# A tuned perceiver layer: who asks for the experts' weights, how many pairs are held at a time, and where the gathered results go

## The chip, the cores and the metric

The kernel runs on one core of a Trainium2 chip. The metric is the device time of one execution in microseconds (us), the median over several runs. Engines are TensorE (PE; PEld is its weight load), VectorE (DVE), ScalarE (ACT), GpSimd (POOL) and SyncE (SP). All numbers are float32.

## The reference, cut to what matters

One layer has three parts, each added to the 256 x 512 latents `x`: attention of the latents over themselves and 4096 context rows, a state-space mixer, and a mixture of experts. The change lies in the last part:

```
x      = layernorm(latents)                        # 256 tokens, 512 wide
scores = sigmoid(x @ gate_w)                       # 32 experts
w, i   = top_k(scores, 6);  w = w / sum(w)
routed = sum over the 6 experts e of a token: w_e * ((silu(x @ wg[e]) * (x @ wu[e])) @ wd[e])
shared = (silu(x @ sg) * (x @ su)) @ sd
out    = latents + routed + shared
```

An expert has 512 x 192 weights for `wg`, as many for `wu`, and 192 x 512 for `wd`.

## The kernel before, in words

The kernel is written in a tile framework: the programmer allots tiles from pools and writes the instructions; the framework sets each engine's order and all semaphores. `tc.issue_after(i)` puts an engine's instructions behind `i` on the same engine. Each engine runs its own list in order.

**Attention and mixer** take the first 785 us or so. Their tile `xn` (2 x 512 values per partition) holds normalised rows, in between the target of ACT's sums of squares (line 282) and the zeros that are written to DRAM; `xT` (4 x 256) is its transpose, in between room for sums.

**Routing** (from about 785 us). `route`, `ranks` and `counts` give each token's six experts. `places` orders the 24 experts behind the first eight by how many tokens they have and draws them into 24 slots; the slot's expert number comes out of a matmul into `ps_place`, is copied to `expert` (line 1272) and turned by `place_rows` into row numbers `place` for gathers. `result_rows` finds where a token's results will stand (`row_y`), and `list_later` which tokens belong to a block (`listed`).

**Units.** The 32 experts are worked off as 16 pairs, here called units 0 to 15 (`NP`). Units 0 to 3 are the eight fixed experts; 4 to 15 are drawn at run time. A unit's weights are two tiles of 1024 KB, one for each expert (gate, up and the first 128 rows of down; `WEX` = 2048 values per partition), and one of 256 KB with the remaining down rows of both. `NHELD` = 6 places in SBUF hold the weights of six units; the places are buffers of finished work, collected by `hold`. `load_pair(n)` puts unit n's weights into place n mod 6. For the fixed experts SyncE copies them (`load_weights`, line 1406); for the drawn ones GpSimd issues three indirect gathers through `place` (`rows_at`, line 1394).

**The loop** (lines 1765 to 1803) does in round n: `gate_up(n)` (L237 for units 0 to 4, whose two experts have separate blocks of 128 token rows; L1629 for units 5 to 15, whose two experts share one block), `fetch` of token rows (`xg_sb`, gathers on GpSimd from DRAM `xd`), `turn(n + 1)` (TensorE transposes L1601, DVE copy `xgT` L1603), `down(n - 1)` (L1700, L1703, or L1651, L1652), `load_pair(n - 1 + NHELD)`, and `turn_hidden(n)`. Units 4 and 5 are loaded before the loop.

**Results.** Up to unit 10 a block's result `y_sb` is stored to DRAM `ye` by ACT's queue (L1708, L1660). The last five units (from `LAST` = 11) stay on chip: `spread` adds them into `total` by a matmul (L1670). The stored ones are gathered back per token, six gathers `yk` for each of two token tiles (L1557), and added to `x_sb` with their weight on DVE (L1565, `add_behind`). The first tile's six use the pool `yp` of six buffers; the second tile's use four of the same and two of `xg`'s. At the end `finish` adds `total` (L1811) and SyncE stores the output (L1814). If an expert has more tokens than its block has room (`crowded`), another, slower arm runs; the profiled execution did not take it.

Of the kernel before, what the change touches and what calls it, by code (L numbers as in the profile page):

```python
# [23 lines left out]
KD = DM // P  # L24
# [42 lines left out]
NSLOT = NE - FIXED  # L67
# [17 lines left out]
def perceiver_layer(ctx: ExitStack, tc: tile.TileContext, a: dict, out: bass.AP):  # L85
    nc = tc.nc
# [35 lines left out]
    ident = const.tile([P, P], FP, name="ident")  # L122
# [27 lines left out]
    def layer(ctx, bounded):  # L150
# [6 lines left out]
        keep = ctx.enter_context(tc.tile_pool(name="keep", bufs=1))  # L157


        xn = keep.tile([P, NT, DM], FP, name="xn")  # L160
        xT = keep.tile([P, KD, L], FP, name="xT")
        oacc = keep.tile([P, NT, NKV, REP * P], FP, name="oacc")
        lacc = keep.tile([P, NT, NKV, REP * P], FP, name="lacc")

# [3 lines left out]
        row = keep.tile([P, NT, TOPK], U32, name="row")  # L168
        row_y = keep.tile([P, NT, TOPK], U32, name="row_y")
        place = keep.tile([P, NPL], U32, name="place")  # L170
        listed = keep.tile([P, NB], U32, name="listed")
        token = keep.tile([P, NT], FP, name="token")
        crowded = keep.tile([1, 1], I32, name="crowded")
# [1075 lines left out]

        def places(pc):  # L1250

            pos, key, keys, at, value, drawn = (
                m[n] for n in ("pos", "key", "keys", "at", "value", "dst"))
# [12 lines left out]
            ps = bank("ps_place")  # L1266
            TE.matmul(ps[:, 0:n], number, slot[:, 0:n], start=True, stop=True)
            V.tensor_tensor(drawn[:, :, 0:n + 1], m["table"], two(slot, n + 1), ALU.mult)
            V.tensor_reduce(value, drawn[:, :, 0:n + 1], AX.X, ALU.add)
            V.tensor_tensor(drawn, two(ident[:, 0:NE], NE), value.unsqueeze(2).to_broadcast([P, 2, NE]), ALU.mult)  # L1270
            TE.matmul(ps[:, NE:3 * NE], ones, drawn.rearrange("p a b -> p (a b)"), start=True, stop=True)
            V.tensor_copy(expert, ps[:, 0:n])
            place_rows()
            V.tensor_copy(m["base"], ps[:, NE:3 * NE].rearrange("p (a b) -> p a b", b=NE))
# [117 lines left out]
        def rows_at(out, src, c, by=place):  # L1392

            return G.indirect_dma_start(out=out, out_offset=None, in_=src,  # L1394
                                        in_offset=bass.IndirectOffsetOnAxis(ap=by[:, c:c + 1], axis=0)).ins
# [6 lines left out]
        def load_weights(to, n, fixed, behind=None):  # L1402

            if fixed:
                for i in range(2):
                    wait_for(nc.sync.dma_start(to[i], a["experts"][2 * n + i]), behind)
                nc.sync.dma_start(to[2], a["down_rest"][2 * n:2 * n + 2].rearrange("e p n -> (e p) n"))
            else:
                s = 2 * n - FIXED
                for i in range(2):  # L1410
                    rows_at(to[i], a["experts"].rearrange("e p n -> (e p) n"), s + i)
                return rows_at(to[2], a["down_rest"].rearrange("e p n -> (e p) n"), NE - FIXED + s // 2)

        def load_pair(n, behind=None):
            if n < NP:
                k = n % NHELD
                weights[n] = (held[2 * k], held[2 * k + 1], rests[k])
                return load_weights(weights[n], n, 2 * n < FIXED, behind)

# [129 lines left out]

        def gather(src, rows, t, rings):

            got = []
            for k, (pool, tag) in enumerate(rings):
                yk = pool.tile([P, DM], FP, tag=tag, name="yk")
                G.indirect_dma_start(out=yk, out_offset=None, in_=src,  # L1557
                                     in_offset=bass.IndirectOffsetOnAxis(ap=rows[:, t, k:k + 1], axis=0))
# [150 lines left out]

        with ExitStack() as rctx:  # L1710
            main = Rounds(rctx, weights)
            yp = rctx.enter_context(tc.tile_pool(name="yp", bufs=6))
            idx, rowf, sc, rank, mask, iota = (m[n] for n in ("idx", "rowf", "gate", "rank", "mask", "iota"))
            spread, = carve(m["kv", 0], (TAIL // 2, L))

# [31 lines left out]

            for n in range(2):
                begun = main.fetch(n)
            for n in range(FIXED // 2, NHELD):  # L1750
                with tc.issue_after(begun):
                    begun = load_pair(n)
            copied = main.turn(0)
            with tc.issue_after(copied):
                rows_in_blocks(at)
            fetched = {0, 1}
            got, r_x, r_k = [], [(main.e4, "xg")], [(yp, "yk")]

            def add_behind(n, k0, k1):

# [4 lines left out]
            for n in range(NP):  # L1765
                gate_up(n)
                if n == 0:
                    list_later(main.ps_x.tile([P, KD * P], FP, tag="x", name="ps_list"))

                for f in range(n + 2, NP):  # L1770
                    if f not in fetched and sum(main.blocks(b) for b in range(n + 1, f + 1)) <= 4:
                        with tc.issue_after(begun):
                            begun = main.fetch(f)
                        fetched.add(f)

                if n + 1 < NP:
                    main.turn(n + 1)
                if 0 < n <= LAST:
                    down(n - 1)
                elif n > LAST:  # L1780
                    main.down_here(n - 1)
                if n == LAST:
                    got.append(gather(ye, row_y, 0, r_k * TOPK))
                elif n == LAST + 1:
                    total = [main.ps_ye.tile([P, DM], FP, tag="ye", name="total") for _ in range(NT)]
                    got.append(gather(ye, row_y, 1, r_k * 4 + r_x * 2))
                if n > LAST + 1:
                    spread_last(n - 2)
                if n >= NP - 3:
                    add_behind(n, *{NP - 3: (0, TOPK), NP - 2: (TOPK, 2 * TOPK - 2), NP - 1: (2 * TOPK - 2, 2 * TOPK)}[n])  # L1790
                if n > 0:
                    load_pair(n - 1 + NHELD)
                if n == 0:
                    with tc.issue_after(begun):
                        for z in main.zeroed:
                            G.memset(z, 0.0)
                    with tc.issue_after(main.done[n]):
                        room()
                if n == 2:
                    with tc.issue_after(main.done[n - 1]):  # L1800
# [19 lines left out]
            with arms.Else():  # L1820
# [2 lines left out]
                dst, row2f, row2 = m["dst"], m["m8"][:, :, 0:TOPK], row_y  # L1823
                xg_rows = dram_disjoint_views(xg, NT * TOPK)
                for t in range(NT):
                    V.tensor_scalar(dst[:, t], iota[:, 0:NE], float(L), None, ALU.mult)
                    V.tensor_tensor(dst[:, t], dst[:, t], rank[:, t], ALU.add)
                    V.tensor_tensor(own[:, 0:TOPK], m["hot"][:, t], dst[:, t].unsqueeze(1).to_broadcast([P, TOPK, NE]), ALU.mult)
                    V.tensor_reduce(row2f[:, t, :], own[:, 0:TOPK], AX.X, ALU.add)
                    V.tensor_copy(row[:, t, :], row2f[:, t, :])  # L1830
                    for k in range(TOPK):
                        G.indirect_dma_start(
                            out=xg_rows[t * TOPK + k], in_=xn[:, t, :], in_offset=None,
                            out_offset=bass.IndirectOffsetOnAxis(ap=row[:, t, k:k + 1], axis=0))
# [15 lines left out]
                V.tensor_scalar(row2f, row2f, float(NE * L), None, ALU.min)  # L1850
                V.tensor_copy(row2, row2f)
                for t in range(NT):
                    add(gather(ye2, row2, t, [(main.e4, "xg")] * TOPK), t)
                    store(t)

    flag = nc.values_load(small_scores, min_val=0, max_val=1)
# [54 lines left out]
```

## Time and profile before

| what | us |
|---|---|
| median of 3 runs | 940.52 (939.85 to 940.58) |
| the profiled execution | 946.23 |
| its span, first to last instruction | 944.3 |
| TensorE busy | 924.2 |
| first L237 of unit 0 | starts at 810.04 |
| first L1629 (unit 5) | starts at 860.66 |
| last `total` matmul ends | 937.90 |

The span is 1.9 us shorter than the profiled execution's own time. A profile line such as `L1629 PE MATMUL ps_egu<-w_in,xgT` reads: line of the kernel, engine, operation, tile written, tiles read. In a timeline the brackets behind an instruction tell how long its engine was idle before it and what released it. In the chain of waits each piece has its start, its length and what ran.

### The profile page before, as it was taken

The numbers are of one execution on the slowest core, as the hardware profiler recorded it, in microseconds if no ns is written. First come the engines' busy times: TensorE is split into PE (matmuls) and PEld (weight loads), VectorE is DVE, ScalarE is ACT, GpSimd is POOL, SyncE is SP. The second block draws the span as 40 slices with busy tenths as digits, with TensorE's granted clock in tenths as the row PEclk, the third lists the DMA queues.
The fourth block names the chain that finished last, engine by engine and source line by source line (L and its number), as shares of the span: only waits on it lengthen the run. The fifth ranks groups of instructions, "written<-read, shape, count | busy, mean of one in ns | idle before, by whom it ended". The sixth has DMA issues, their size and how long they took to land.

```text
span 944.3 us, 10567 instructions
## 1 busy us (share of the span) xinstructions
PE 924.2 (98%) x3266; PEld 504.9 (53%) x3266; DVE 577.4 (61%) x1199; ACT 370.0 (39%) x853; POOL 427.8 (45%) x498
## 2 busy tenths in 40 slices
PE   7999999999999999999999999999999999999996
PEld 3444555555555555555555555554465775654332
DVE  4866766566666665756666656658588685661224
ACT  4556444344344343443444434434154442022121
POOL 3769846345544644724725544220013251545542
PEclk9999999999999999999999999999999999999999
DMA  9651053053024114204305203090025481779983
GB/s 331 203 112 58 1 179 89 1 154 92 1 66 146 33 31 159 57 3 154 90 0 157 68 1 89 14 298 1 0 101 197 145 309 68 288 287 348 421 330 101
DMA packets 129716, 122.33 MB, mean 130 GB/s; under 512 B 79889, under 2 KB 99122, under 8 KB 124402
## 3 DMA queue, kind: packets, MB, share of 16 engines
q1 hardware_dynamic: 118960, 77.43, 27.2%
q0 software_dynamic: 7504, 39.59, 11.3%
q10 hardware_dynamic: 3186, 4.54, 1.3%
q8 instruction: 28, 0.46, 0.2%
q14 instruction: 38, 0.31, 0.1%
HBM read 89.54 MB, written 32.00 MB: 129 GB/s over the span
## 4 chain that ended last, share of the span: by engine, by line
PE 96%; DVE 2%; DMA 0%; issue 0%; ACT 0%; POOL 0%; SPq 0%; ACTq 0%
PE oT L774 24%; PE scT L748 24%; PE ps_kv L522 16%; PE ps_self L237 4%; PE ps_egu L1629 3%; PE ps_o L969 3%; PE ps_egu L237 3%; PE ps_first L399 3%; PE ps_xbc L237 2%; PE ps_out L1163 1%; PE ps_z L237 1%; PE xgTp L1601 1%; PE ps_ye L1651 1%; PE ps_ye L1652 1%; PE total L1670 1%; PE ps_ye L1700 1%
## 5 line engine op out<-in xcount | busy, mean ns | idle before, releaser
L765 DVE TENSOR_TENSOR lacc<-lacc,prT 128x512 f32<-128x512 f32 x256 | 199.8, 781 | 198.0 <-ACT prT L754 196.6
L754 ACT ACTIVATE prT<-scT,bq,rk 128x512 f32<-128x512 f32 x256 | 198.4, 775 | 280.9 <-PE scT L748 268.8
L748 PE MATMUL scT<-qT,kT 128*128 128x512 f32 x536 | 273.5, 592 | 0.0
L774 PE MATMUL oT<-prT,v 128*128 128x512 f32 x528 | 269.4, 592 | 0.0
L774 PEld LDWEIGHTS oT<-prT,v 128*128 128x128 f32 x528 | 100.2, 190 | 125.3 <-issue 118.6
L748 PEld LDWEIGHTS scT<-qT,kT 128*128 128x128 f32 x536 | 101.3, 190 | 41.4 <-issue 30.8
L522 PE MATMUL ps_kv<-fast,ctx 128*128 128x256 f32 x350 | 99.5, 379 | 0.0
L522 PEld LDWEIGHTS ps_kv<-fast,ctx 128*128 128x128 f32 x350 | 66.5, 190 | 47.9 <-issue 39.9
L471 POOL TENSOR_TENSOR ctx<-ctx 128x128 f32<-128x128 f32 x21 | 10.4, 495 | 98.7 <-PE ps_kv L522 98.7
L211 POOL TENSOR_TENSOR rk<-pv,mhalf 128x4 f32<-128x4 f32 x32 | 38.7, 1219 | 27.3 <-DVE pv L210 27.1
L522 PE MATMUL ps_kv<-wkv,ctx 128*128 128x256 f32 x168 | 48.8, 379 | 0.0
L282 ACT ACTIVATE xn<-kraw 128x128 f32<-128x128 f32 x112 | 33.5, 301 | 38.5 <-POOL kraw L497 21.5
L507 POOL TENSOR_TENSOR v<-fast,v 128x768 f32<-128x768 f32 x21 | 40.8, 1958 | 16.5 <-DVE fast L551 15.9
L522 PEld LDWEIGHTS ps_kv<-wkv,ctx 128*128 128x128 f32 x168 | 31.9, 190 | 28.2 <-issue 24.6
L780 DVE TENSOR_TENSOR oacc<-oT,oacc 128x512 f32<-128x512 f32 x64 | 43.7, 682 | 0.0
L1394 POOL DMA_INDIRECT xg_sb<-xd,listed x21 | 20.1, 959 | 31.7 <-DVE lacc L1258 14.4
L522 PE MATMUL ps_kv<-fast,fast 128*128 128x256 f32 x112 | 33.3, 379 | 0.0
L1633 DVE TENSOR_TENSOR hid<-si,ps_egu 128x128 f32<-128x128 f32 x11 | 3.2, 288 | 47.0 <-ACT si L1631 40.0
L522 PEld LDWEIGHTS ps_kv<-fast,fast 128*128 128x128 f32 x112 | 21.3, 190 | 17.8 <-issue 12.0
L288 DVE STREAM_TRANSPOSE tr<-kraw 128x512 f32<-128x512 f32 x28 | 18.3, 690 | 19.6 <-POOL kraw L496 19.6
L469 POOL TENSOR_TENSOR ctx<-fast 128x128 f32<-128x128 f32 x28 | 20.4, 730 | 19.6 <-PE ps_kv L522 19.1
L969 PE MATMUL ps_o<-wo,qT 128*128 128x512 f32 x64 | 28.8, 592 | 0.0
(423 smaller groups left out, 1399.9 us busy)
## 6 DMA issues: line engine op xcount, KB each, us to landing
xg<-xn SPq DMA_DIRECT2D x6, 2560.0 KB
ctx<-in_ctxT_dram SPq DMA_DIRECT2D x7, 1024.0 KB, 4.7
kd<-tr SPq DMA_DIRECT2D x112, 64.0 KB, 2.2
kT<-kd SPq DMA_DIRECT2D x28, 256.0 KB, 2.8
wq<-in_wq_dram SPq DMA_DIRECT2D x4, 1024.0 KB, 10.4
wo<-in_wo_dram SPq DMA_DIRECT2D x4, 1024.0 KB
w_in<-in_W_inT_dram SPq DMA_DIRECT2D x4, 1024.0 KB, 11.7
w_in<-in_experts_dram SPq DMA_DIRECT2D x4, 1024.0 KB, 6.9
```

Of the source, the lines that this page charges most:

```text
L211: return G.tensor_tensor(dst, v[:, :n], mhalf[:, :n], ALU.pow)
L237: last = TE.matmul(ps, lhs(k), rhs_of(k), start=(k == 0), stop=(k == KD - 1))
L282: S.activation(sq[:, h, :], raw[:, h, :], AF.Square, accum_out=ss[:, h:h + 1])
L399: TE.matmul(ps, lhs[:, j, k, :], rhs[:, k, :], start=(start and k == 0), stop=(k == 1), skip_group_check=True)
L507: G.tensor_tensor(to[:, 1:4], q, base[:, 1:4], ALU.add)
L522: TE.matmul(b[n], sets[name][i], y, start=start, stop=True, skip_group_check=True)
L748: scored.append(TE.matmul(sc, kT[:, g, i * P:(i + 1) * P], qT[:, t, heads4(g), :].rearrange("p h q -> p (h q)"), start=True, stop=True).ins)
L754: S.activation(pr, sc, AF.Exp, bias=shift, scale=SCALE if r is None else r[:, i, g:g + 1])
L765: V.tensor_tensor(la, la, pr, ALU.add)
L774: TE.matmul(outs[g, t], v[:, i, g * HD:(g + 1) * HD], pr, start=(n == 0), stop=last)
L780: V.tensor_tensor(ov, outs.pop((g, t)), ov, ALU.add)
L969: TE.matmul(m["ps_o", t], aT[:, t, h, :], wo[j][:, h % 4, :], start=(h == 0), stop=(h == NH - 1))
```

## The change

1. For units 4 to 15 the second expert's 1024 KB are copied by SyncE: it reads the expert's number from a new one-row tile `drawn` into a register and copies from that address. The first expert and the 256 KB remainder are still gathered by GpSimd. `drawn` is written by one more DVE copy in `places`.
2. A seventh place. `xn` and `xT` become the halves of one tile `latents`, which is as large as one expert's weights; the six result buffers become one tile `yks`, whose first part holds the second expert and whose next part the remainder. Unit 6 uses this place once. Units 4, 5 and 6 are loaded before the loop; round n (1 to 6) loads unit n + 6, round 7 loads nothing, rounds 8 to 10 load units 13 to 15.
3. The results come back by six gathers in round 11 (into `yks`), two in round 12 (into `latents`) and four in round 13 (into `yks` again).
4. In the crowded arm `xn` is read back from `xd` first.

The diff, cut to its core:

```diff
-        xn = keep.tile([P, NT, DM], FP, name="xn")
-        xT = keep.tile([P, KD, L], FP, name="xT")
+        latents = keep.tile([P, 2, KD * L], FP, name="latents")
+        xn = latents[:, 0].rearrange("p (t d) -> p t d", t=NT)
+        xT = latents[:, 1].rearrange("p (k n) -> p k n", k=KD)
...
+        drawn = keep.tile([1, NSLOT], I32, name="drawn")
...
+            V.tensor_copy(drawn, ps[0:1, 0:n])
             V.tensor_copy(expert, ps[:, 0:n])
...
                 s = 2 * n - FIXED
-                for i in range(2):
-                    rows_at(to[i], a["experts"].rearrange("e p n -> (e p) n"), s + i)
+                _, e = nc.values_load_multi_w_load_instructions(drawn[0:1, s + 1:s + 2], engines=[mybir.EngineType.SP], min_val=0, max_val=NE - 1)
+                nc.sync.dma_start(to[1], a["experts"][bass.ds(e[0], 1)].rearrange("o p n -> (o p) n"))
+                rows_at(to[0], a["experts"].rearrange("e p n -> (e p) n"), s)
                 return rows_at(to[2], a["down_rest"].rearrange("e p n -> (e p) n"), NE - FIXED + s // 2)
...
-                k = n % NHELD
+                k = n if n <= NHELD else (n - 1) % NHELD
...
-            yp = rctx.enter_context(tc.tile_pool(name="yp", bufs=6))
+            yks = rctx.enter_context(tc.tile_pool(name="yks", bufs=1)).tile([P, TOPK * DM], FP, name="yks")
+            held.extend((latents.rearrange("p a n -> p (a n)"), yks[:, 0:WEX]))
+            rests.append(yks[:, WEX:WEX + DM])
...
-            for n in range(FIXED // 2, NHELD):
+            for n in range(FIXED // 2, NHELD + 1):
...
-            got, r_x, r_k = [], [(main.e4, "xg")], [(yp, "yk")]
+            got, r_x = [], [lambda: main.e4.tile([P, DM], FP, tag="xg", name="yk")]
+            r_k = [lambda k=k: yks[:, k * DM:(k + 1) * DM] for k in range(TOPK)]
+            r_l = [lambda k=k: latents.rearrange("p a (b n) -> p (a b) n", n=DM)[:, k] for k in range(2)]
...
-                    got.append(gather(ye, row_y, 0, r_k * TOPK))
+                    got.append(gather(ye, row_y, 0, r_k))
...
-                    got.append(gather(ye, row_y, 1, r_k * 4 + r_x * 2))
+                    got.append(gather(ye, row_y, 1, r_l))
...
+                if n == NP - 3:
+                    got[1] += gather(ye, row_y, 1, r_k[0:TOPK - 2], 2)
-                if n > 0:
-                    load_pair(n - 1 + NHELD)
+                if n > 0 and n != NHELD + 1:
+                    load_pair(n + NHELD - (n > NHELD))
...
+                for t in range(NT):
+                    nc.sync.dma_start(xn[:, t, :], xd[t * P:(t + 1) * P, :])
```

More of the change, by code (lines that the diff above doesn't have):

```diff
@@ L1250, in places @@
         def places(pc):
-            pos, key, keys, at, value, drawn = (
+            pos, key, keys, at, value, each = (
                 m[n] for n in ("pos", "key", "keys", "at", "value", "dst"))
@@ L1267, in places @@
             TE.matmul(ps[:, 0:n], number, slot[:, 0:n], start=True, stop=True)
[L1268 to L1271, printed above, removed]
+            V.tensor_tensor(each[:, :, 0:n + 1], m["table"], two(slot, n + 1), ALU.mult)
+            V.tensor_reduce(value, each[:, :, 0:n + 1], AX.X, ALU.add)
+            V.tensor_tensor(each, two(ident[:, 0:NE], NE), value.unsqueeze(2).to_broadcast([P, 2, NE]), ALU.mult)
+            TE.matmul(ps[:, NE:3 * NE], ones, each.rearrange("p a b -> p (a b)"), start=True, stop=True)
+            V.tensor_copy(drawn, ps[0:1, 0:n])
             V.tensor_copy(expert, ps[:, 0:n])
@@ L1544, in layer, with gather @@
         actx.close()
-        def gather(src, rows, t, rings):
+        def gather(src, rows, t, places, k0=0):
             got = []
-            for k, (pool, tag) in enumerate(rings):
-                yk = pool.tile([P, DM], FP, tag=tag, name="yk")
+            for k, place_of in enumerate(places, k0):
+                yk = place_of()
                 G.indirect_dma_start(out=yk, out_offset=None, in_=src,
@@ L1852, in layer @@
                 for t in range(NT):
-                    add(gather(ye2, row2, t, [(main.e4, "xg")] * TOPK), t)
+                    add(gather(ye2, row2, t, r_x * TOPK), t)
                     store(t)
```

## The prediction

> **What bounds the kernel now.** I read first the page's busy table and its 40 slices.
>
> ```profile
> span 944.3 us, 10567 instructions
> PE 924.2 (98%) x3266; PEld 504.9 (53%) x3266; DVE 577.4 (61%) x1199; ACT 370.0 (39%) x853; POOL 427.8 (45%) x498
> ...
> DMA  9651053053024114204305203090025481779983
> ```
>
> TensorE is busy for 924.2 of 944.3 us, so all that any edit outside TensorE can return is the 20.1 us left, 6.4 of them behind the last matmul. The change lives in the last 140 us (the experts), where the DMA digits reach 9. The next view is the busy time by stage, whose last columns are granted clock, DMA share and GB/s.
>
> ```profile
> 811.00:814.00 3.00, 3.00 (x10) 1.71 (x9) 2.93 (x11) 0.33 (x1) 2.09 (x4) 1.00 1.02 415
> ...
> 817.00:820.00 3.00, 3.00 (x22) 3.00 (x22) 1.31 (x5) 0.04 (x1) 1.16 (x2) 0.75 1.00 415
> 820.00:823.00 3.00, 3.00 (x7) 1.64 (x7) 2.38 (x5) 0.44 (x1) 2.77 (x6) 0.68 0.94 345
> ...
> 826.00:829.00 3.00, 3.00 (x8) 1.00 (x7) 2.34 (x8) 0.38 (x2) 1.42 (x2) 1.00 0.05 19
> ...
> 877.00:882.00 5.00, 4.40 (x36) 1.42 (x36) 1.33 (x4) 1.29 (x3) 3.23 (x4) 1.00 1.02 424
> ...
> 907.00:910.00 3.00, 3.00 (x20) 1.21 (x14) 0.73 (x2) 0.86 (x2) 0.00 (x0) 1.00 1.02 423
> ```
>
> The transfers are full at about 415 to 424 GB/s from 811 to 823 and from 868 to 910, and nearly empty at 826 to 829. TensorE is hardly short of work in any of them: full transfers are not yet late weights. Which wait ends last is in the chain of waits (start, length, what):
>
> ```profile
> 867.11 2.72 PE ps_egu L1629 x32
> ...
> 872.68 2.72 PE ps_egu L1629 x32
> ...
> 875.99 1.47 PE ps_ye L1651 x8
> 877.48 0.34 ACT si L1631
> ...
> 878.54 0.70 DVE xgT L1603
> 879.29 2.79 PE ps_egu L1629 x32
> ...
> 923.18 1.61 PE hidTp L1641 x2
> ...
> 935.23 2.67 PE total L1670 x6
> ```
>
> No piece of this chain is a weight transfer. A unit costs 5.57 us from one L1629 start to the next (867.11 to 872.68); units 7, 8 and 9 cost 6.61, 6.16 and 6.51, and unit 10 5.65, together 2.65 us over. There ACT's `si` starts at 877.48 though the matmuls that it reads end before 875.4. Another 2.06 us go at 923.4, where TensorE waits for ACT's `y_sb`. These 4.7 us are the only stalls inside the stage that look as if relief of the transfers could return them. But the profiled execution took 946.23 us, 5.71 more than the median of 940.52, so most of the 4.7 may exist only while profiling.
>
> Last, the gathers of GpSimd (start, length, idle before and its releaser):
>
> ```profile
> 819.79 0.95 POOL L1394 DMA_INDIRECT xg_sb<-xd,listed  x1 [0.30 <-PE xgTp L1601]
> ...
> 900.17 0.94 POOL L1394 DMA_INDIRECT ctx<-in_experts_dram,place  x1 [1.48 <-DMA v<-in_down_rest_dram,place]
> ...
> 911.83 0.95 POOL L1557 DMA_INDIRECT yk<-ye,row_y  x1 [8.21 <-DMA ye<-y_sb]
> ```
>
> The last weights are asked for at 900.2 to 901.4 and used at 926.6, the transfers being drained by about 912: over 14 us to spare. GpSimd waits, but nobody on the chain waits for it.
>
> **The change part by part.** A unit's weights are 2 x 1024 KB + 256 KB = 2.36 MB.
>
> *The extra copy of `drawn`.* One DVE copy of 1x24 goes ahead of L1272, which is on the chain (806.28, 0.18 us). Neighbouring rows start 0.10 us apart (L1272 at 806.28, L1274 at 806.38), and a lone one takes 0.18: +0.10 to +0.18, I take +0.10.
>
> *GpSimd to SyncE.* Twelve gathers of 0.94 us and their 0.30 us of issue leave GpSimd, 15 us, none on the chain: 0. SyncE has no 1 MB copy left behind 783, so twelve copies meet an empty queue. The register read's nearest row is L1802 on SP: a load of 0.29 us at 822.5, register work and an assert, done by 823.1, so 0.6 us, and 0.33 us for a copy's issue (L1406). One pair per unit of 5.57 us or more leaves SyncE over 80% idle. New waits: each copy waits for its place, freed by the previous `down`; behind it SyncE has only later copies, the `crowded` read and, at 937.86, the output stores. No compute engine waits for that read at its turn. Cost 0; without that cover 0.9 us per unit, 11 us in all.
>
> *Bandwidth.* From 808 to 811 the row shows 190 GB/s while GpSimd issues one gather per 1.25 us, so there issue limits and SyncE can fill up to (415-190) x 3 = 0.67 MB, 1.6 us of full transfer. From 868 to 910 share is already 1.0. [...]
>
> *The seventh place.* Unit 6 is asked for at once, about 808 to 815, and units 7 to 12 one unit earlier; unit 7 asks for nothing, units 13 to 15 as before. So 2.36 MB move from the full stretch at 878 to the opening one. The gain: the drain at 912 comes 2.36/0.42 = 5.6 us earlier, the results' gathers (911.83) up to 4 us earlier. The last addition ends at 932.0, 5 us before its use at 937.1, and the last two are held behind unit 15's hidden values (929.8) anyway: 0.
>
> The price: the token rows of unit 2 (issued 818.5 and 819.8) stand behind the additional copies. Before them now go 4.72 MB, with themselves 5.24. Summing the rows from 808 (0.57 MB to 811, then 415, 429, 415, 345 GB/s) passes 5.24 at 822.6. Afterwards 7.60 MB must pass: at 415 GB/s from 820 that is 827.8, or 826.2 if SyncE fills the 0.67 MB. Their transposes start at 828.84. Completion costs more than bytes: a result gather issued 911.83 is used at 915.26, 3.4 us, of which 256 KB at 199 GB/s are 1.3, so up to 2.1 us besides. Landing lies between 826.2 and 829.9: TensorE waits 0 to 1.1 us; most of the interval is before 828.84, so I take +0.3.
>
> *Results six, two, four.* The same 12 gathers of 1.25 us. Now four of the second tile's wait for buffers; afterwards two go at once and four wait for the first additions one unit later. Bounds -0.5 to +0.5 through DVE's order near 920 (an addition is 0.75 us and two stand between unit 14's multiplies, but `hidTp` there starts only after `total` at 923.18): 0.
>
> *One tile for `xn` and `xT`.* Their bytes stay apart; 0 unless waits go by whole tiles.
>
> Sum: 0.10 + 0 + 0.3 + 0 = +0.4. Against its own time: 946.23 to 946.6; carried to the median of unprofiled runs, 940.52 to 940.9. A difference of 0.2% (1.9 us) is about what a measurement of this kernel can tell from no change.
>
> **The rivals.** *Stalls are real and go away (faster).* If the 2.65 us of units 7 to 10 and the 2.06 at 923 come from the full transfers and also happen unprofiled, dropping unit 7's load just at 878 removes most: between half and all, -2.4 to -4.7, with +0.1 to +0.4 on top, about 937.3 (936.0 to 938.6). For it: they begin inside the full stretch. Against: units 11 and 12, also full (423 GB/s), cost 5.57 and 5.59; and the profiled run's surplus of 5.71 covers them.
>
> *Unit 2's rows come late (slower).* Place: the transposes at 828.84. It decides from 1.9 us of lateness, or less if the clock drops too. If two queues together reach only the 345 of 820 to 823, 7.60 MB pass at 831.4, land by 833.5: 4.7 us late. Clock: granted 0.75 and 0.68 in the two rows of 817 to 823 cost 3 x 0.25 + 3 x 0.32 = 1.7 us, after an idle of only 1.16 us at 808.9; a second such stretch costs the same. So +1.9 to +6.4, typically +2.8: 943.3. For it: idle and clock loss stand side by side in this very stage. Against: the margin computed above. [...]
>
> *Whole-tile waits (slower).* If `latents` is tracked as one, 28 groups of squares into `xn` (L282) would queue with `xT`'s sums all through attention; at 0.2 us for each, +5.6, 946.1. Nothing in the trace of before speaks for it: halves of `xn` already live apart.
>
> *It does not do what it says:* if SyncE's copies are issued late, weights still have over 14 us: within the likeliest case.
>
> **How the numbers follow.** Likeliest, nothing measurable: 0.45, 940.9, its own range 939.0 to 942.4. Faster: 0.25. Slower: late rows 0.25 plus whole tiles 0.05. The range to 937.0 leaves out under a third of the faster case (0.07); to 944.3 it leaves out a third of late rows (0.08) and the tiles (0.05): 0.20 outside.
>
> **What would show it.** Right: SP copies near 808, 809, 810; no load at unit 7; DMA share below 1 near 880 and drained near 906; the first result gather near 908; TensorE's wait before the transposes at 829 under 1.1 us; stage length from 810 within 1.9 us. Faster is right if spacings of units 7 to 10 fall to 5.6 and unprofiled time follows. Wrong: a wait of 2 us or more on `xg_sb` near 829, half clock after it, or longer attention.

## The result, and the profile after

The changed kernel takes 946.26 us (946.17 to 946.38, 4 runs) against 940.28 (939.85 to 940.58, 4 runs) before: a ratio of 1.0064 [1.0047, 1.0082], about 6 us slower. The two profiled executions hide this, 946.38 against 946.23, because the one of before was slow by itself; experiment 1 gives a second profile of the kernel before, which is used from here on.

The page of the changed kernel, its busy table and the DMA slices:

```profile
span 944.6 us, 10641 instructions
...
PE 923.3 (98%) x3266; PEld 505.1 (53%) x3266; DVE 577.8 (61%) x1200; ACT 370.1 (39%) x853; POOL 417.4 (44%) x486
...
DMA  9651053053024114204305303180036481989973
```

TensorE's work is what it was (923.3 us against 924.2), GpSimd has 10 us less. Against experiment 1's profile (922.7 us busy of 939.0) TensorE is busy 0.6 us more and idle 5.0 us more. So the 6 us are time in which TensorE has nothing to do or runs slowly. Busy time by stage, the last columns being granted clock, DMA share and GB/s:

```profile
808.00:811.00 3.00, 2.15 (x10) 1.26 (x8) 2.93 (x9) 0.00 (x0) 2.23 (x3) 1.00 0.90 191
811.00:814.00 3.00, 3.00 (x11) 1.79 (x10) 2.97 (x11) 0.33 (x1) 2.25 (x3) 1.00 1.00 423
817.00:820.00 3.00, 3.00 (x15) 2.93 (x15) 1.43 (x5) 0.16 (x1) 1.83 (x2) 0.52 1.00 411
820.00:823.00 3.00, 3.00 (x10) 1.70 (x9) 1.70 (x5) 0.42 (x2) 2.53 (x7) 0.91 1.01 416
823.00:826.00 3.00, 3.00 (x10) 1.49 (x8) 0.58 (x3) 0.56 (x2) 0.50 (x1) 1.00 1.03 419
826.00:829.00 3.00, 0.25 (x1) 0.00 (x0) 0.93 (x5) 0.00 (x0) 1.09 (x1) 1.00 1.04 384
829.00:832.00 3.00, 2.33 (x10) 1.24 (x10) 1.66 (x3) 0.00 (x0) 0.00 (x0) 0.80 0.99 363
832.00:835.00 3.00, 3.00 (x9) 1.09 (x9) 2.86 (x9) 0.48 (x1) 0.20 (x1) 0.64 0.61 158
877.00:882.00 5.00, 5.00 (x48) 1.87 (x44) 1.33 (x4) 0.83 (x3) 1.50 (x2) 1.00 1.02 422
```

From 826 to 829, where the transfers were nearly empty before (0.05, 19 GB/s), they are now full (1.04, 384 GB/s), and TensorE works for 0.25 of 3 us. Behind it the clock falls a second time, to 0.80 and 0.64. TensorE's timeline at that place (start, length, what, and in brackets the idle time before it):

```profile
825.23 1.02 PE L1704 MATMUL ps_ye<-w_in,hidT 128*128 128x512 f32 x2
829.67 1.27 PE L1605 MATMUL xgTp<-ident,xg_sb 128*128 128x128 f32 x8 [3.43 <-DMA xg_sb<-xd,listed]
830.76 1.90 PE L1704 MATMUL ps_ye<-w_in,hidT 128*128 128x512 f32 x2
832.59 1.90 PE L1707 MATMUL ps_ye<-v,hidT 64*128 64x512 f32 x4
834.42 0.55 PE L1694 MATMUL hidTp<-ident,hid 128*128 128x128 f32 x3
834.80 2.75 PE L239 MATMUL ps_egu<-w_in,xgT 128*128 128x384 f32 x8
```

TensorE idles 3.43 us for unit 2's token rows. The order is new: the transposes (L1605) stand behind one matmul of `down(0)`, and the rest of `down(0)` behind them. Nothing in the diff asks for that; the framework made it. The chain of waits shows the same transfer, and the later units:

```profile
817.86 11.68 DMA xg_sb<-xd,listed
...
876.11 2.72 PE ps_egu L1633 x32
881.69 2.72 PE ps_egu L1633 x32
887.26 2.72 PE ps_egu L1633 x32
```

Units 7 to 10 now stand 5.57 us apart. The results are gathered back no earlier (GpSimd's timeline):

```profile
912.52 0.94 POOL L1561 DMA_INDIRECT yks<-ye,row_y  x1 [12.67 <-issue]
```

That is 8.61 us behind the start of unit 12 (903.91); in the second profile of the kernel before it is 8.26 (908.31 against 900.05).

### The profile page after: what moved, and what is told of

Same layout as the page of the kernel before. It is cut to its first block, busy times and chain, and to the rows that moved or that the text cites. A ratio compares the mean times of both kernels' runs of the same rounds, so it can differ in the third digit from the quotient of the medians.

```text
span 944.6 us, 10641 instructions
## 1 busy us (share of the span) xinstructions
PE 923.3 (98%) x3266; PEld 505.1 (53%) x3266; DVE 577.8 (61%) x1200; ACT 370.1 (39%) x853; POOL 417.4 (44%) x486
## 4 chain that ended last, share of the span: by engine, by line
PE 94%; DVE 2%; DMA 2%; ACT 0%; issue 0%; POOL 0%; ACTq 0%
PE oT L776 24%; PE scT L750 24%; PE ps_kv L524 16%; PE ps_self L239 4%; PE ps_egu L1633 3%; PE ps_o L971 3%; PE ps_egu L239 2%; PE ps_first L401 2%; PE ps_xbc L239 2%; PE ps_out L1165 1%; PE ps_z L239 1%; DMA xg_sb<-xd,listed 1%; PE ps_ye L1656 1%; PE ps_ye L1655 1%; PE xgTp L1605 1%; PE total L1674 1%
## 5 line engine op out<-in xcount | busy, mean ns | idle before, releaser
L284 ACT ACTIVATE latents<-kraw 128x128 f32<-128x128 f32 x112 | 33.5, 301 | 38.6 <-POOL kraw L499 21.5
L524 PEld LDWEIGHTS ps_kv<-fast,fast 128*128 128x128 f32 x112 | 21.3, 190 | 17.9 <-issue 12.0
L239 PE MATMUL ps_self<-wq,latents 128*128 128x512 f32 x64 | 28.6, 592 | 0.0
```

The source lines that it names most:

```text
L239: last = TE.matmul(ps, lhs(k), rhs_of(k), start=(k == 0), stop=(k == KD - 1))
L284: S.activation(sq[:, h, :], raw[:, h, :], AF.Square, accum_out=ss[:, h:h + 1])
L524: TE.matmul(b[n], sets[name][i], y, start=start, stop=True, skip_group_check=True)
```

## The experiments

They ran on several chips, four, four, three, four and three at a time (1 to 4, 5 to 8, 9 to 11, 12 to 15, 16 to 18); the kernel before ran beside each group and took 940.24, 939.91, 942.59, 940.20 and 942.04 us. So ratios are compared, not times; a ratio is formed from all executions, not from the two medians. Five numbers matter for each run, the last four from its profile:

| kernel | ratio to before, interval | idle before unit 2's transposes | unit 2 starts | unit 14 to last `total` | behind it |
|---|---|---|---|---|---|
| 1 before, second profile | 1.0002 [0.9992, 1.0011] | 0 | 830.88 | 19.55 | 6.4 |
| changed kernel | 1.0064 [1.0047, 1.0082] | 3.43 | 834.80 | 20.45 | 7.3 |
| 2 `down(0)` first | 1.0043 [1.0023, 1.0063] | 2.84 | 831.02 | 20.69 | 7.2 |
| 3 unit 6 later | 1.0006 [0.9996, 1.0016] | 0 | 829.91 | 20.78 | 7.4 |
| 4 SyncE alone | 1.0011 [1.0001, 1.0020] | 0 | 828.49 | 21.27 | 7.3 |
| 5 wait filled | 1.0050 [1.0034, 1.0067] | 0.78 | 833.50 | 20.16 | 7.3 |
| 6 new order alone | 0.9993 [0.9983, 1.0003] | 0 | 829.86 | 19.55 | 6.4 |
| 7 seven places, no SyncE | 1.0038 [1.0023, 1.0052] | 0 | 834.23 | 20.42 | 8.0 |
| 8 results alone | 1.0020 [1.0010, 1.0030] | 0 | 830.54 | 19.55 | 8.2 |

The last two columns are in us: from the first gate and up matmul of unit 14 to the end of the last `total` matmul, and from there to the end of the span.

The starts of unit 2 hold one thing that comes and goes with the execution. In 9 of the 20 profiles (the first of the kernel before, the changed kernel, 1, 3, 5, 6, 14, 16, 18) TensorE has a stretch at half clock near 817 to 821; in the other 11 it has none. Where the clock was read by the microsecond, in the first six of the nine, the stretch is 3.4 us long (0.88, 0.50, 0.50, 0.50 and 0.91 from 817 to 822 in experiment 1); in 14, 16 and 18 four transposes near 819 take 1.06 us as in 1, against 0.60 in the 11. Experiments 10 and 18 are one kernel, and only 18 has it. It costs 1.4 us here: from the start of unit 0 to the start of unit 2 the three profiles of the kernel before, all with this early half clock, take 21.26 us, and experiments 8, 11 and 15, which have the same order without it, 19.88. By this measure the changed kernel takes 25.50 (with it), experiment 6 20.07 (with it), experiment 2 22.06 (without) and experiment 7 24.17 (without). A start of unit 2 can be compared only between profiles that are alike in this.

**1. The kernel before, once more.** No edit.

> The kernel before, unchanged, with a second profile. If its 2.65 us over 5.57 in units 7 to 10 and the 2.06 us at 923 exist only while profiling, the timed median is 940.3 to 940.5 again, and the new profile shows stalls of other size or place, or none, and its own time moves by as much (between 940.5 and 947). If they are real stalls of the kernel they come back at the same places with the same sizes, the profiled time is again near 946.2 while the timed median is 940.4.

940.55 us. The new profile spans 939.0 us, and its chain has no stall:

```profile
866.68 2.72 PE ps_egu L1629 x32
872.25 2.72 PE ps_egu L1629 x32
877.83 2.72 PE ps_egu L1629 x32
883.40 2.72 PE ps_egu L1629 x32
```

Every distance is 5.57 or 5.58 us. The usual execution has none of the stalls of units 7 to 10, so relief of the transfers has nothing to return there. They are not confined to one execution, though: the profile of experiment 11, which executes the same work as the kernel before, has two of them, 6.64 us from unit 7 to unit 8 (871.00 to 877.64) and 6.09 to unit 9. Its order around unit 2, on TensorE's timeline:

```profile
825.55 1.88 PE L1700 MATMUL ps_ye<-w_in,hidT 128*128 128x512 f32 x4
827.36 1.12 PE L1703 MATMUL ps_ye<-v,hidT 64*128 64x512 f32 x2
828.41 1.10 PE L1601 MATMUL xgTp<-ident,xg_sb 128*128 128x128 f32 x8
829.44 1.12 PE L1703 MATMUL ps_ye<-v,hidT 64*128 64x512 f32 x2
830.49 0.55 PE L1690 MATMUL hidTp<-ident,hid 128*128 128x128 f32 x3
```

Between this profile and the changed kernel's lie 5.6 us, in three places of the table: 834.80 - 830.88 = 3.92 up to unit 2, 20.45 - 19.55 = 0.90 from unit 14 on, 7.3 - 6.4 = 0.9 (0.86 before rounding) behind the last matmul.

**2. The changed kernel in the order of before.** Unit 2's transposes are pinned behind all of `down(0)`.

```diff
-                if n + 1 < NP:
+                if n + 1 < NP and n != 1:
                     main.turn(n + 1)
...
+                if n == 1:
+                    with tc.issue_after(main.last_down):
+                        main.turn(n + 1)
```

> The changed kernel, with unit 2's transposes pinned behind all of down(0) on TensorE, as the kernel before has them; the rows still land late. Theory A (the 6 us are the wait for unit 2's rows and the half clock behind it): the transposes are now needed near 829.2 instead of 826.2, the wait falls from 3.43 us to 0.3 to 1, the 0.64 clock goes if the idle is short: 941.5 to 943.5. If the clock drops even after a short wait, 943 to 945. Theory B (SyncE's copies make every unit's transfers slower, the order matters little): 945 to 946.5.

942.74 us, 2.5 more than before, but with a wide spread: six of the ten executions took 941.1 to 942.9 us at a mean granted clock of 0.996 to 0.998, four took 945.2 to 948.8 at 0.994 or 0.995 (the changed kernel's four: 946.2 to 946.4, three of them at 0.994). So the ratio, 1.0043, stands for about 4 us. The profile is of one of the six; how the four lost their time no profile shows.

```profile
825.33 1.13 PE L1707 MATMUL ps_ye<-v,hidT 64*128 64x512 f32 x4
829.30 0.63 PE L1605 MATMUL xgTp<-ident,xg_sb 128*128 128x128 f32 x4 [2.84 <-DMA xg_sb<-xd,listed]
830.23 0.63 PE L1605 MATMUL xgTp<-ident,xg_sb 128*128 128x128 f32 x4 [0.31 <-DMA xg_sb<-xd,listed]
```

The rows land as late as in the changed kernel. The wait is 2.84 us and not the 0.3 to 1 expected, because in this execution the clock did not fall at 818, and TensorE began `down(0)` 2.0 us earlier (823.52 against 825.55); no half clock follows either (1.00 from 826 to 835). Unit 2 starts at 831.02, only 0.14 later than in experiment 1, but that profile has the early half clock. From unit 0 to unit 2 it is 22.06 us against the 19.88 of experiments 8, 11 and 15, so the late rows cost 2.18 here; the changed kernel has 25.50 against the 20.07 of experiment 6, with the same order and the same early half clock, so 5.43 there. The old order does not make late rows free. How much of the lateness counts depends on the order and on whether a half clock follows.

**3. Unit 6's weights behind unit 2's rows.** All else of the change stays.

```diff
-            for n in range(FIXED // 2, NHELD + 1):
+            for n in range(FIXED // 2, NHELD):
...
+                if n == 0:
+                    rows_of_two = begun
+                    with tc.issue_after(begun):
+                        begun = load_pair(NHELD, ...)
```

> The changed kernel, with unit 6's three transfers issued only behind the token rows of unit 2 (SyncE's copy too); SyncE still does half of the weights, the seventh place and the results stay. Theory A (late rows): rows land 5 us earlier or more, no wait on xg_sb near 829 and no second half clock: 940.0 to 941.0. Theory B (SyncE's copies are the cost): 945 to 946.5.

940.82 us. The transposes stand even further ahead, and the rows are there:

```profile
825.78 1.04 PE L1605 MATMUL xgTp<-ident,xg_sb 128*128 128x128 f32 x8
826.66 1.88 PE L1704 MATMUL ps_ye<-w_in,hidT 128*128 128x512 f32 x4
```

So the early load of unit 6 delays the rows, and with it gone 5.4 of the 6 us go. SyncE's copies are still all there: they are not the cost.

**4. SyncE's copies alone**, with six places (the diff's lines on `drawn` and `load_pair`, nothing else).

> The kernel before with SyncE copying the second expert of units 4 to 15 through its register, and nothing else: six places, the results as before. Theory A (the seventh place's early load is the cost): 940.0 to 941.0, with the rows of unit 2 in time. Theory B (SyncE's copies are the cost): 944 to 947.

941.29 us, 0.3 above theory A's range. Theory B is out. What little is lost is lost at the end: unit 2 starts 2.39 us earlier than in experiment 1, where the clock had fallen, and unit 15 still 2.3 (918.79 against 921.13), but the chain then runs through the results' gathers:

```profile
906.24 6.50 DMA yk<-ye,row_y
921.08 3.69 DMA yk<-ye,row_y
929.49 2.67 PE total L1673 x6
```

**5. The wait filled with work.** The changed kernel with 24 transposes of a constant ahead of unit 2's; the order is pinned to the changed kernel's.

```diff
+                    if n == 2 and i == 0 and blocks is None:
+                        for k in range(24):
+                            TE.transpose(tp[:, k % KD, :], ident, ident)
```

> The changed kernel with the same order on TensorE, and 24 additional transposes of the constant ident (about 3.1 us at 0.13 us each) between its first matmul of down(0) and unit 2's transposes, so that TensorE is busy while it waits for the rows. Theory A1 (of the 6 us, 1.65 are the half clock that follows the idle stretch): the rows still land near 829.6, the clock stays at 1.00 from 830 to 834, and the time falls by about 1.65 us: 944.4 to 944.9. Theory A2 (all of it is the wait, the clock would have dropped anyway): 946.0 to 946.6, with 0.5 in the rows of 830 to 834 again.

944.45 us. TensorE's timeline, and then two rows of busy time by stage:

```profile
826.36 2.78 PE L1606 MATMUL xgTp<-ident 128*128 128x128 f32 x24
829.93 1.34 PE L1608 MATMUL xgTp<-ident,xg_sb 128*128 128x128 f32 x8 [0.78 <-DMA xg_sb<-xd,listed]
```

```profile
829.00:832.00 3.00, 2.17 (x12) 1.11 (x10) 2.68 (x7) 0.00 (x0) 0.94 (x1) 1.00 1.04 388
832.00:835.00 3.00, 3.00 (x13) 1.64 (x13) 3.00 (x13) 1.37 (x3) 2.08 (x2) 1.00 0.87 287
```

The rows land no earlier, but the clock stays at 1.00, and unit 2 starts 1.3 us earlier than in the changed kernel (both profiles have the early half clock). So in the profiles the second half-clock stretch is a real part of the loss, and it goes when the idle time is filled. The ratios point the same way, 1.0050 against 1.0064, but their intervals overlap.

**6. The new order alone.** The kernel before, with the changed kernel's order around unit 2 (the transposes pinned behind the first matmul of `down(0)`, the rest behind them).

> The kernel before, with the changed kernel's order on TensorE around unit 2: one matmul of down(0), unit 2's transposes, the rest of down(0). Theory A (the order costs only because the rows are late): rows land before they are needed, no wait, and since the four 64-row matmuls stand together again (1.06 us for four, against 1.05 for two where before has split them), 939.0 to 940.3. Theory C (the order itself costs, whatever the rows do): 942 or more.

939.47 us, 0.9993 [0.9983, 1.0003].

```profile
825.73 1.02 PE L1702 MATMUL ps_ye<-w_in,hidT 128*128 128x512 f32 x2
826.58 1.04 PE L1601 MATMUL xgTp<-ident,xg_sb 128*128 128x128 f32 x8
827.46 1.02 PE L1702 MATMUL ps_ye<-w_in,hidT 128*128 128x512 f32 x2
828.41 1.13 PE L1709 MATMUL ps_ye<-v,hidT 64*128 64x512 f32 x4
```

With early rows the new order costs nothing; its four 64-row matmuls stand together (1.06 us to the next start; in experiment 1 each half of them takes 1.05), and unit 2 starts 1.02 us earlier. Experiments 1, 2, 6 and the changed kernel make a square: rows early, old order 1.0002; rows early, new order 0.9993; rows late, old order 1.0043; rows late, new order 1.0064. The late rows are needed for the loss; the order changes its size in the profiles, though the intervals of the last two ratios overlap. (The two kernels with late rows also hold the losses at the end of the table.)

**7. Seven places without SyncE.** `load_pair` gathers all as before; the rest of the change stays.

> The changed kernel with all weights gathered by GpSimd: the seventh place and the results six, two, four stay, SyncE copies nothing. TensorE has all of down(0) and down(1), about 6 us of work, ahead of unit 2's transposes here. Theory A (late rows cost only where the order needs them): rows near 830 to 832, a wait of 0 to 1.5 us, 940.3 to 942. Theory B' (the additional 2.36 MB at the opening cost 5 us in any order): 945 to 947. The stretch from the end of the last total matmul to the end of the span: 6.4 to 6.5 us as in the kernel before if SyncE's register work sets the 7.2 to 7.4 of the kernels with it, 7.3 if not.

943.96 us, more than theory A allowed. Here the framework put all of `down(0)` and `down(1)` ahead of the transposes: the rows are not waited for, unit 2 starts at 834.23, but unit 3 at 841.62, only 0.32 later than in experiment 1, since `down(1)` is already done. Experiment 1 has the early half clock, however, and 7 has not. The nearest kernel is that of experiment 8, which lacks only the seventh place and has no early half clock either: from unit 0 to unit 3 it takes 30.31 us, and 7 takes 31.56. So 1.25 us are lost there. What the profile loses otherwise lies in the last two columns, 0.87 and 1.5 us against experiment 1. The price of late rows depends on what stands before them: 1.25 us with this order, 5.43 with that of the changed kernel.

**8. Results six, two, four alone**, with the joined tiles and the read-back in the crowded arm, six places, no SyncE.

> The kernel before with the joined tiles and the results gathered six, two, four, and nothing else. If the result order costs what the changed kernel loses in its last unit (0.85 us between the start of unit 15 and the end of the last total matmul, 12.23 against 11.38): 940.9 to 941.3, and that stretch is 12.2. If that loss comes from later gathers or another order on VectorE that go with SyncE: 940.0 to 940.5, and the stretch is 11.4.

942.08 us, more than either case. Up to the last matmul nothing is lost (19.55), but 8.2 us follow it, not 6.4. The read-back alone has as large a ratio (experiment 11, 1.0021), so the order of the results shows no cost of its own.

**9 and 10. Two more additions behind the last `hid`**, in the kernels of 4 and 3.

```diff
-                    add_behind(n, *{..., NP - 2: (TOPK, 2 * TOPK - 2), NP - 1: (2 * TOPK - 2, 2 * TOPK)}[n])
+                    add_behind(n, *{..., NP - 2: (TOPK, TOPK + 2), NP - 1: (TOPK + 2, 2 * TOPK)}[n])
```

> The kernel of e4 (SyncE's copies, six places) with four instead of two of the last additions behind the last hid on VectorE. Theory D (the 2.3 us that e4 holds at the start of unit 15 are lost because VectorE has the additions of the ninth and tenth result, and so the landing of a late gather, ahead of the last hid): the stretch from unit 15 to the end of the last total matmul falls from 13.36 to about 11.4 us, the time from 941.3 to 939.2 to 939.8. Theory E (the gathers themselves end the kernel): the stretch stays above 13 and the time at 941 or more.

1.0001 [0.9982, 1.0020], and the stretch from unit 14 is 24.64 us in a profile in which TensorE waits 2.68 us for `hidT` at 921; between the theories this one decides nothing. But it bears on the clock: behind this wait the matmuls take nearly twice their time, the two of L1655 2.07 us from 925.17, against 1.12 at 907.39 and 1.13 at 931.24.

```profile
923.72 0.66 PE L1654 MATMUL ps_ye<-w_in,hidT 128*64 128x512 f32 x1 [2.68 <-ACT hidT L1647]
```

> The kernel of e3 (the changed kernel with unit 6 loaded behind unit 2's rows) with the same four additions behind the last hid. Theory D: the last stretch falls from 12.23 to about 11.4 and unit 14 to 15 from 8.55 to 8.2; 940.8 becomes 939.6 to 940.1. Theory E: no change, 940.8.

940.80 us beside 942.59 for the kernel before, 0.9979 [0.9966, 0.9992]. But unit 15 to the end still takes 12.23 us, and the stretch from unit 14 20.60. Theory D is wrong as to the place; why the ratio is better see 16 and 18.

**11, 14 and 15. Code that is not executed.** The kernel before with the change's fourth part alone, two copies in the arm that does not run.

```diff
+                for t in range(NT):
+                    nc.sync.dma_start(xn[:, t, :], xd[t * P:(t + 1) * P, :])
```

> The kernel before with the two copies of xn in the crowded arm, which is not executed, and nothing else. If the stretch behind the last total matmul (6.4 us in the kernel before, 7.2 to 8.1 in the kernels that hold parts of the change) depends on where the code lies, it can move here too, by up to 1.6 us, and the time with it: 940.3 to 942. If it depends on what is executed: 6.3 to 6.5 us, and 940.3.

1.0021 [1.0004, 1.0038], and 7.9 us behind the last matmul. 14 and 15 put both kernels on one chip:

> The kernel before, once more, for one profile on the chip of these runs. Stretch behind the last total matmul 6.3 to 6.5 us if it belongs to the kernel, 7.2 to 8.1 if it belongs to the chip. Stalls beyond 5.57 us in units 7 to 10: none if they belong to single executions, as in the second profile.

> The kernel of e11 (before, with two copies added in the arm that is not executed), once more beside the kernel before on the same chip. If the place of the code sets the stretch behind the last total matmul, it is again 7.9 us here and 6.4 in the kernel before; if not, both are alike.

The stores at the end of the kernel before, with the span that heads the answer:

```profile
core 0 of [0], span 939.6 us
...
933.21 1.13 SPq L1814 DMA_DIRECT2D out_dram<-x_sb  x2
```

and of the kernel with the added code:

```profile
core 0 of [0], span 938.9 us
...
930.97 1.13 SPq L1814 DMA_DIRECT2D out_dram<-x_sb  x2
```

From the issue of the stores to the end it is 6.4 us in the one and 7.9 in the other, on the same chip. Over all profiles this stretch goes with the kernel: 6.4 in four profiles of kernels without SyncE's copies and without the read-back, 7.2 to 7.4 in twelve with SyncE's copies, 7.9 to 8.2 in four with the read-back and no SyncE. So the stretch can grow by 1.5 us without one more executed instruction. The 0.9 us of the changed kernel come with SyncE's copies (7.3 us in experiment 4 too, which has no read-back); whether these cost them as work that is done or as code that is added no run separates. Which of the instructions at the end is late the profile does not show. (14 has no stall in units 7 to 10 either.)

**12 and 13. Additions behind unit 14's `hid`**, in the kernel of 3 and in the changed kernel.

> The kernel of e3 with VectorE's additions reordered: one instead of six ahead of unit 14's hid, the next seven behind it, the last four behind unit 15's hid. Theory F (in the changed kernel the six additions that wait for gathers hold back unit 14's hid and the copy xgT of unit 15, and TensorE has to do two of the total matmuls later): the stretch from unit 14's start to the end of the last total matmul falls from 20.78 us in e3 (20.45 in the changed kernel) to the 19.55 of the kernel before, and the time from 1.0006 of the kernel before to 0.9990 to 0.9996 of it. Theory G (the stretch is longer because the gathers themselves end later): it stays at 20.4 to 20.8, the ratio at 1.000 to 1.001.

> The changed kernel with the same reordered additions and nothing else. Theory F: stretch 19.55 instead of 20.45, 0.9 us off the changed kernel, a ratio of about 1.0054 to the kernel before instead of 1.0064. Theory G: 20.4, ratio 1.006 or more. The wait of about 3.4 us before unit 2's transposes is there in both.

1.0028 [1.0018, 1.0037] and 1.0088 [1.0069, 1.0107]. In both, the last four gathers were issued before three of the additions that had to read the same buffers first: these three add other rows, so the result is wrong, and wait for the last gathers. They do not answer the question. 13 shows the wait once more, 4.67 us before unit 2's transposes, with a slow stretch behind it: the eight transposes take 1.94 us, against 1.04 in experiment 3.

**16, 17 and 18. The same, mended, and 10 again.**

```diff
-                    add_behind(n, *{NP - 3: (0, TOPK), NP - 2: (TOPK, 2 * TOPK - 2), NP - 1: (2 * TOPK - 2, 2 * TOPK)}[n])
-                if n == NP - 3:
+                    add_behind(n, *{NP - 3: (0, 1), NP - 2: (1, TOPK + 2), NP - 1: (TOPK + 2, 2 * TOPK)}[n])
+                if n == NP - 2:
                     got[1] += gather(ye, row_y, 1, r_k[0:TOPK - 2], 2)
```

> As e12 was meant: the kernel of e3, VectorE with one instead of six additions ahead of unit 14's hid, and the last four gathers issued in round 14, behind the additions that free their buffers (in e12 and e13 they stood ahead of three of these additions, which so added the wrong rows and waited for the last gathers). Theory F: the stretch from unit 14's start to the end of the last total matmul 19.55 us instead of 20.78 in e3, the time 0.9990 to 0.9996 of the kernel before. Theory G (late gathers set the end): 20.4 or more, 1.000 or more.

> The changed kernel with that order of additions and nothing else. Theory F: the stretch is 19.55 instead of 20.45, the ratio to the kernel before about 1.0054. Theory G: 20.4 or more, 1.006 or more. The wait of 3.4 us for unit 2's rows stays in both.

> The kernel of e10 on another chip: is it faster than the kernel before (0.9979 there, where the kernel before took 942.6) or the like (e3, from which it differs by two additions, was 1.0006)? If the ratio is a property of the kernel: 0.997 to 0.999. If it was that chip: 1.000 to 1.001.

16: 940.77 us, 0.9984 [0.9975, 0.9992]. 17: 946.00 us, 1.0038 [1.0024, 1.0053]. 18: 941.01 us, 0.9986 [0.9976, 0.9996]. The stretch from unit 14 is 20.28 in 16 (20.78 in 3) and 21.22 in 17 (20.45 in the changed kernel). Theory F wanted 19.55 in both, so it is wrong; theory G fits the stretch of 17 and misses that of 16 by 0.1 us, and its ratios (1.000 or more, 1.006 or more) fit neither. The ratio of 17 is lower than the changed kernel's because the kernel before is slower on this chip: 17's own time is about that of the changed kernel, 946.26. The 0.9 us from unit 14 on stay unexplained. 17 shows the wait again:

```profile
823.66 1.02 PE L1704 MATMUL ps_ye<-w_in,hidT 128*128 128x512 f32 x2
828.87 2.02 PE L1605 MATMUL xgTp<-ident,xg_sb 128*128 128x128 f32 x8 [4.19 <-DMA xg_sb<-xd,listed]
```

10, 16 and 18 are faster than the kernel before by 0.14 to 0.21%, on the two chips where that kernel took 942.0 and 942.6. Their own times, 940.8 to 941.0, are those of experiment 3 on a chip where before took 940.2. So a version that beats both kernels is shown on these two chips only.

## Why the prediction was wrong, point by point

**The step that failed: when unit 2's rows are needed.** The working took 828.84 from the trace of before. The landing it derived, 826.2 to 829.9, holds, near its late end: the transposes start on the rows at 829.67 in the changed kernel and at 829.30 in experiment 2 (830.02 in 13). But in the changed kernel TensorE is free for the transposes at 825.23 + 1.02 = 826.25, because half of `down(0)` now stands behind them. 829.67 - 826.25 is the wait of 3.43 us, against the 0 to 1.1 of the working and the +0.3 taken. That the framework would order the instructions anew was not considered, though the text counted every transfer. And 828.84 was no fixed time even in the old order: the profile that it was read from has the early half clock, and without it the same transposes start at 827.23 and 826.91 (experiments 11 and 15). So in experiment 2, with the old order and no early half clock, TensorE still waits 2.84 us.

**The clock.** The rival "unit 2's rows come late" had the mechanism and the place, a wait and a second stretch at half clock, and its range, +1.9 to +6.4, holds the measured 6. Part of that is luck: it had the rows land by 833.5 because it let two queues reach only the 345 GB/s of 820 to 823, and they landed at 829.54 with 384 to 429 GB/s from 811 to 829. Experiment 5 took the stretch away and unit 2 started 1.3 us earlier; the ratio went from 1.0064 to 1.0050. At this place the second stretch came after 3.43, 4.19 and 4.67 us of idle time (the changed kernel, 17 and 13: clock 0.50 from 831 to 834, 0.50 from 829 to 832, and 1.94 us for eight transposes), and none came after 2.84 or 0.78 (2 and 5: clock 1.00 from 826 to 835). It is not so everywhere: in experiment 9 matmuls at about half speed follow a wait of 2.68 us, so the length of the idle time alone does not decide. The first stretch, near 817 to 821, is another matter: it appears in 9 of 20 profiles and is missing in 11, with much the same idle time near 809 (0.85 to 1.16 us). So the row from which the prediction took its clock loss, a drop after little idle time, was real too, but it does not tell when the clock drops. In one-microsecond windows of the changed kernel the clock is 0.89, 0.50, 0.50, 0.50 and 0.91 from 830 to 835, which makes 3.4 us at half clock for the second stretch as for the first.

**The sum at unit 2.** Against experiment 6, which has the same order: TensorE is free 0.33 us earlier (826.25 against 826.58), waits 3.43, and then needs 5.13 us to unit 2's start instead of 3.28, half clock included: -0.33 + 3.43 + 1.85 = 4.95, and the starts differ by 834.80 - 829.86 = 4.94. The new order by itself gives 1.02 back, so 3.92 remain against the kernel before.

**Terms put at 0 that were not.** The end: 0.9 us from unit 14 on, in every kernel with SyncE's copies or the seventh place of the table (20.2 to 21.3 against 19.55), cause open; and 0.9 us behind the last matmul, in every kernel with SyncE's copies, cause open too (11, 14 and 15 show only that this stretch can grow without an executed instruction). 3.92 + 0.90 + 0.86 - 0.06 between units 2 and 14 = 5.62; the spans differ by 5.6.

**Terms that held.** The copy of `drawn` costs 0.10 us (805.84 to 805.94 on VectorE). GpSimd to SyncE brings nothing (experiment 4: 1.0011), and 877 to 882 runs at 422 GB/s against 424: issuing from two queues added no bandwidth here, as the row said (share 1.0 from 868 to 910). At 808 to 811 it added none either: 191 GB/s against 190, at a share of 0.90 against 0.65, so the 0.67 MB that SyncE was to fill in there, and with them the early bound of 826.2, did not come. The drain came earlier (910 to 915: share 0.26, against 0.95 in experiment 1).

**Details that were wrong and cost nothing.** The transfers at 880 are as full as before. The results' gathers did not start earlier. In the kernel before they wait for unit 10's stores, which the line shown there said (`8.21 <-DMA ye<-y_sb`). The changed kernel's line names no releaser, but its first gather stands 8.1 us behind the issue of the last of these stores (904.41), as against 7.8 in experiment 1 (900.55), so the same wait is likely.

**The other rivals.** "Stalls are real and go away": units 7 to 10 did lose their stalls in the profile, but experiments 1 and 14 show none to lose. The argument that the surplus of 5.71 us covers them held for the median; that they exist only while profiling is not shown, since the profiled execution of experiment 11 has two of them at 943.01 us, the second lowest of its ten. "Whole-tile waits": its 0.2 us for each group was the author's estimate; the first gate matmul starts at 784.23 against 784.25, so attention is no longer.

## What to carry to other kernels

When a transfer is moved ahead of another, do not compare its new landing with the old time of use: a framework that schedules may move the use as well, so ask which work can slip behind it. Give small transfers that the next step needs their place before large ones that are needed late: putting one unit's weights behind 512 KB of token rows returned 5.4 of the 6 us. And take a profile of the kernel before that agrees with its median before explaining any stall in it.

## What was not expected of the hardware

A wait for data can cost more than its length: 3.43 us of idle time brought another 3.4 us at half clock, and with the wait filled by useless transposes unit 2 started 1.3 us earlier. The length does not tell it alone: 2.68 us brought matmuls at about half speed in experiment 9 (2.07 us for two that else take 1.12), and 2.84 us none in experiment 2 (clock 1.00). An early half clock that costs 1.4 us comes and goes between executions and moves later starts with it: from unit 0 to unit 5 it is 50.54 us with it in experiment 1, and 49.18 without in 11. Late data can also cost less than they are late: in experiment 7 unit 2 starts 4.3 us later than in experiment 8, counted from unit 0, and unit 3 only 1.25. And two copies in an arm that never runs lengthened the end of the kernel by 1.5 us, on two chips.
